# GpSimd's order by hand, one power for several tiles, and a row written to DRAM in 16-byte pieces

One of the cores of a Trainium2 chip runs the whole program. The metric is the device time of one launch in microseconds, the median of several runs; "the kernel before" and "the changed kernel" are the two compared.

## The reference

Two layers over 32 graphs ("batches") of 512 nodes with 512 features and one 512 x 512 adjacency matrix, all in f32. Layer 0 is pre-normalised attention with 8 heads under the adjacency as a mask; layer 1 is a graph attention layer. Cut to what matters:

```python
h = jnp.maximum(_layernorm(x, axis=-1), 0.0)                 # layer 0
q, k, v = h @ Wq + bq, h @ Wk + bk, h @ Wv + bv              # 8 heads of 64
scores = q k^T / 8 + (1.0 - adj) * -1e9
x = x + softmax(scores) @ v @ Wo + bo

h0 = jnp.maximum(_layernorm(x, axis=-1), 0.0)                # layer 1
h = h0 @ W;  s1, s2 = h @ a1, h @ a2
e = leaky_relu(s1[:, :, None] + s2[:, None, :], 0.2) * adj
att = softmax(e, axis=2)
x = x + elu(att @ h + beta * h)
```

## The kernel before

The kernel is software-pipelined over batches. One step of the main loop does, in TensorE's order, the parts of the string `0VD1G2YN3WKQ`: score tiles of head pairs 0 to 3 (digits; each digit also does the products with `v` of the pair before), `V` values, `D` the row sums of layer 1 (`pe`), `G` gather, `Y` layer 1's output, `N` the next batch's transposes, `W` the attention's output projection, `K` and `Q` the next batch's projections. The projections use seven block products instead of eight, fed by sums of blocks ("combinations", `combos`) that GpSimd makes. In the views a product is named after its PSUM tile (`x`, `y` or `qz`) and its part: `y_w` is a product of W, `qz_k` one of K.

TensorE's and VectorE's instructions stand in the order in which the program emits them; the others are placed by the framework's scheduler:

```python
BY_HAND = {mybir.EngineType.PE, mybir.EngineType.DVE}
```

VectorE's small work is put off with `later(key, wait, cost, fn)`, which emits `fn` when a rough clock says that TensorE would not be held up by it.

The combinations; `tT` are those of V, K and Q, `uT` those of W:

```python
def combos(b, name, pairs):
    b11, b12, b21, b22 = (block(pairs, k) for k in range(4))
    t2, t3, t4 = (wtile([P, 2, H], f"{name}{i}_{b}", "T", 5) for i in (2, 3, 4))
    nc.gpsimd.tensor_tensor(t3, b22, b12, op=ALU.subtract)
    nc.gpsimd.tensor_tensor(b12, b12, b11, op=ALU.subtract)
    nc.gpsimd.tensor_tensor(t2, b22, b12, op=ALU.subtract)
    nc.gpsimd.tensor_tensor(t4, t2, b21, op=ALU.subtract)     # "the fourth combination"
    ...
```

The other GpSimd work that matters: `es` (six additions a head pair: the sum of the exponentials), the division `oT`, the residual's constant (`c_row`, four additions a batch), and layer 1's row sums `as`:

```python
def residual(b, st, ...):                       # the start of W
    ...
        nc.gpsimd.tensor_tensor(r[:, t, :], r[:, t, :], c_row, op=ALU.add)

def rest(k):                                    # one "at pair" (two VectorE instructions), its share of as
    z = wtile([P, N], f"at_{b}_{k}", "at", 4)
    nc.vector.scalar_tensor_tensor(z, row, s12[:, 1, k : k + 1], adjT[:, k, :], op0=ALU.add, op1=ALU.mult)
    nc.vector.scalar_tensor_tensor(z, z, ALPHA, z, op0=ALU.mult, op1=ALU.max)
    nc.scalar.activation(z, z, AF.Exp)
    ... nc.gpsimd.tensor_tensor(st["as"], st["as"], z, op=ALU.add)      # for k = 1, 2, 3
```

`row` is `s1` of all 512 nodes on every partition. It comes from a [128, 4] tile by way of DRAM, written element by element and read back as a broadcast:

```python
nc.sync.dma_start(d.rearrange("(t p) -> p t", p=P), col, allow_slow_non_contiguous=True)
nc.sync.dma_start(dst, d.unsqueeze(0).to_broadcast([P, N]))
```

## Time and profile before

| | kernel before |
|---|---|
| time, median (lowest to highest) | 4157.85 us (4149.56 to 4160.77, 4 runs) |
| busy share of the profiled span of 4138.1 us | TensorE 90%, VectorE 57%, GpSimd 54%, ScalarE 34% |
| mean granted TensorE clock | 0.953 |

The prediction below shows the waits and the timelines. Two more lines, from the list of DMA issues (out<-in, queue, count, size, median us from issue to landing):

```profile
s<-row_s SPq DMA_DIRECT2D x32, 256.0 KB, 4.7
...
row_s<-s SPq DMA_DIRECT2D x32, 2.0 KB, 8.0
```

Writing 2 KB takes longer than the 256 KB broadcast that follows. It is on the way of `at`, `as` and `pe`.

### The profile page before, as it was taken

The numbers are of one execution on the slowest core, as the hardware profiler recorded it, in microseconds if no ns is written. First come the engines' busy times: TensorE is split into PE (matmuls) and PEld (weight loads), VectorE is DVE, ScalarE is ACT, GpSimd is POOL, SyncE is SP. The second block draws the span as 40 slices with busy tenths as digits, with TensorE's granted clock in tenths as the row PEclk, the third lists the DMA queues.
The fourth block names the chain that finished last, engine by engine and source line by source line (L and its number), as shares of the span: only waits on it lengthen the run. The fifth ranks groups of instructions, "written<-read, shape, count | busy, mean of one in ns | idle before, by whom it ended". The sixth has DMA issues, their size and how long they took to land. (4 is left out here: it accounts for less than half of the span.)

```text
span 4138.1 us, 59294 instructions
## 1 busy us (share of the span) xinstructions
PE 3735.1 (90%) x24162; PEld 1884.2 (46%) x24162; DVE 2373.7 (57%) x3804; ACT 1404.8 (34%) x2085; POOL 2217.4 (54%) x1922
## 2 busy tenths in 40 slices
PE   6899999999999999999999999999999999999955
PEld 4444444455444444444454444454444454444422
DVE  5566555556565565555666555566555566555553
ACT  2333333333333333333333333333333333333321
POOL 4655465455564555565455564555555555554541
PEclk8999999999999999999999999999999999999978
DMA  3001101011101011010011010011010011010010
GB/s 100 29 4 34 34 31 34 3 34 34 34 31 34 4 34 34 31 34 25 12 34 34 31 34 21 17 34 34 31 34 12 26 34 34 31 34 9 18 34 24
DMA packets 83894, 120.87 MB, mean 29 GB/s; under 512 B 24672, under 2 KB 28768, under 8 KB 83616
## 3 DMA queue, kind: packets, MB, share of 16 engines
q1 hardware_dynamic: 78368, 110.98, 8.4%
q10 hardware_dynamic: 4880, 5.24, 0.4%
q8 instruction: 192, 3.15, 0.4%
q0 software_dynamic: 368, 0.79, 0.1%
q14 instruction: 86, 0.70, 0.1%
HBM read 83.37 MB, written 33.63 MB: 28 GB/s over the span
## 5 line engine op out<-in xcount | busy, mean ns | idle before, releaser
L464 DVE TENSOR_TENSOR e<-ps,nmT 128x1024 f32<-128x1024 f32 x384 | 456.9, 1218 | 751.7 <-PE ps L454 751.7
L475 POOL TENSOR_TENSOR es<-e,e 128x512 f32<-128x512 f32 x256 | 321.6, 1278 | 775.2 <-ACT e L468 775.2
L475 POOL TENSOR_TENSOR es<-es,e 128x512 f32<-128x512 f32 x512 | 681.4, 1363 | 0.0
L468 ACT ACTIVATE e<-e 128x1024 f32<-128x1024 f32 x512 | 541.3, 1057 | 326.9 <-DVE e L464 290.1
L454 PE MATMUL ps<-qT,kT 64*128 64x512 f32 x2048 | 495.0, 618 | 73.5 <-DVE e L464 73.4
L483 PE MATMUL po<-e,v 128*64 128x512 f32 x2048 | 502.8, 635 | 0.1
L46 PE MATMUL py<-w,gT 128*64 128x512 f32 x2048 | 453.1, 595 | 11.3 <-DVE y L646 11.3
L46 PE MATMUL pg<-at,hn 128*64 128x512 f32 x2048 | 451.0, 598 | 3.6 <-DVE dmax L619 3.6
L502 DVE RECIPROCAL rd<-pd 128x512 f32<-128x512 f32 x128 | 428.6, 3348 | 6.7 <-POOL oT L506 6.7
L454 PEld LDWEIGHTS ps<-qT,kT 64*128 64x128 f32 x2048 | 183.4, 187 | 372.1 <-issue 189.1
L406 POOL TENSOR_TENSOR qT<-qT,edge 128x256 f32<-128x256 f32 x128 | 90.4, 727 | 420.7 <-DVE qT L402 420.5
L46 PEld LDWEIGHTS py<-w,gT 128*64 128x64 f32 x2048 | 142.4, 137 | 317.5 <-issue 256.3
L46 PEld LDWEIGHTS pg<-at,hn 128*64 128x64 f32 x2048 | 146.1, 138 | 303.5 <-issue 272.2
L483 PEld LDWEIGHTS po<-e,v 128*64 128x64 f32 x2048 | 157.1, 146 | 272.2 <-issue 246.4
L273 POOL TENSOR_TENSOR rs<-rs,mhalf 128x1 f32<-128x1 f32 x256 | 163.5, 644 | 197.3 <-DVE rs L272 196.8
L588 ACT ACTIVATE at<-at 128x512 f32<-128x512 f32 x128 | 80.7, 630 | 450.7 <-DVE at L587 450.7
L517 POOL TENSOR_TENSOR x<-x,c_row 128x512 f32<-128x512 f32 x128 | 160.0, 1271 | 117.4 <-DMA x<-in_x_dram 112.9
L648 POOL TENSOR_TENSOR y<-y,x 128x512 f32<-128x512 f32 x128 | 161.4, 1271 | 110.7 <-DVE y L646 106.5
L496 ACT COPY oT<-po 128x512 f32<-128x512 f32 x128 | 74.4, 581 | 429.3 <-PE po L483 429.3
L645 DVE TENSOR_SCALAR y<-y 128x512 f32<-128x512 f32 x128 | 123.5, 965 | 145.2 <-ACT y L644 145.2
L46 PE MATMUL qz_k<-hT,wk 128*64 128x256 f32 x512 | 88.9, 505 | 121.3 <-DVE x L528 107.5
L592 POOL TENSOR_TENSOR as<-at,at 128x512 f32<-128x512 f32 x32 | 56.8, 1774 | 256.6 <-ACT at L588 256.6
(179 smaller groups left out, 6051.1 us busy)
## 6 DMA issues: line engine op xcount, KB each, us to landing
x<-in_x_dram SPq DMA_DIRECT2D x128, 256.0 KB, 3.0
x<-in_x_dram SPq DMA_DIRECT2D x64, 512.0 KB, 4.6
out_dram<-y SPq DMA_DIRECT2D x128, 256.0 KB, 2.2
s<-row_s SPq DMA_DIRECT2D x32, 256.0 KB, 4.7
adj<-in_adj_dram SPq DMA_DIRECT2D x4, 256.0 KB, 5.6
w<-in_L_gnn_W_dram ACTq DMA_DIRECT2D x1, 1024.0 KB, 7.5
wk<-in_L_gnn_Wk_dram ACTq DMA_DIRECT2D x3, 256.0 KB, 5.1
wq<-in_L_gnn_Wq_dram ACTq DMA_DIRECT2D x3, 256.0 KB, 7.9
```

Of the source, the lines that this page charges most:

```text
L46: nc.tensor.matmul(out[s : s + HD], lhsT[:, s : s + HD], rhs, start=start, stop=stop, skip_group_check=onto)
L273: nc.gpsimd.tensor_tensor(rstd, rstd, mhalf[:, 0:1], op=ALU.pow)
L406: nc.gpsimd.tensor_tensor(qh, qh, edge8[:, ts(k, H)], op=ALU.mult)
L454: nc.tensor.matmul(ps[s], st["kT"][j][rows, ts(k, P)], st["qT"][j][rows, :], start=True, stop=True)
L464: nc.vector.tensor_tensor(e, p, nmT[:, k, :].unsqueeze(1).to_broadcast([P, 2, N]), op=ALU.add)
L468: nc.scalar.activation(e, e, AF.Exp)
L475: nc.gpsimd.tensor_tensor(es[:, s, :], one[:, s, :], e[:, s, :], op=ALU.add)
L483: nc.tensor.matmul(po[s * HD : (s + 1) * HD, :], v[k // 2][:, k % 2, (2 * j + s) * HD : (2 * j + s + 1) * HD], e[k][:, s, :], start=k == 0 ...
L502: nc.vector.reciprocal(rd, st["pd"])
L517: nc.gpsimd.tensor_tensor(r[:, t, :], r[:, t, :], c_row, op=ALU.add)
L645: nc.vector.tensor_scalar(y, y, 1.0, -1.0, op0=ALU.min, op1=ALU.add)
L648: nc.gpsimd.tensor_tensor(y, y, st["x1"][t // 2][:, t % 2, :], op=ALU.add)
```

## The change

Intent: VectorE and TensorE no longer wait for GpSimd at the wrong moment. (1) GpSimd's order is the order of emission. (2) The power -1/2 of layer norm is taken for all four tiles of a batch (layer 0) or two (layer 1) at once, and layer 0's statistics and normalisation go to other places in VectorE's order. (3) `s1`'s row is written as 128 pieces of 16 bytes; that leaves the queries in the order q*4 + t, so the transposed adjacency is stored in it too, and the diagonal, the row sums and `gT` are read with a step of 16 bytes. The core of the diff:

```diff
-BY_HAND = {mybir.EngineType.PE, mybir.EngineType.DVE}
+BY_HAND = {mybir.EngineType.PE, mybir.EngineType.DVE, mybir.EngineType.Pool}
...
+        if mix:
+            nc.sync.dma_start(d.rearrange("(p t) -> p t", t=T), col)
+        else:
+            nc.sync.dma_start(d.rearrange("(t p) -> p t", p=P), col, allow_slow_non_contiguous=True)
...
+    def mixed(ap):
+        return ap.rearrange("p (q t) -> p t q", t=T)
...
-            nc.scalar.copy(adjT[:, k, :], p)
+            nc.scalar.copy(mixed(adjT[:, k, :]), p.rearrange("p (t q) -> p t q", t=T))
...
+    def root(rstd, mv):
+        nc.vector.tensor_scalar_add(rstd, mv[:, :, 1], EPS)
+        nc.gpsimd.tensor_tensor(rstd, rstd, mhalf[:, : rstd.shape[1]], op=ALU.pow)
...                                                            # norm0, layer 0
-            later(("x", b), 1.2, 0.55, lambda: second(t, mv, rstd))
+            if t == T - 1:
+                root(rstd, mv)
+                for u in range(T):
+                    later(("x", b), 10.0, 0.55, lambda u=u: second(u))
...
-            later(("x", b), 6.0, 1.0, lambda t=t: first(t))
+            later(("x", b), wait, 0.95, lambda t=t: first(t))   # wait is 30 for b > 1
...                                                            # norm1, layer 1: two tiles at once
+            if i:
+                root(rstd, mv)
+                later(key, 2.5, 0.4, second)
...
-        as_row(row, s12[:, 0, :], f"s1_{b}")
+        as_row(row, s12[:, 0, :], f"s1_{b}", mix=True)
...
-            later(("at", b), 5.0, 1.45, lambda k=k: rest(k))
+            later(("at", b), 5.5, 1.45, lambda k=k: rest(k))
...
-            product(nc, pd[:, t, :], st["as"][:, ts(t, P)], ones[:, :HD], start=True, stop=True)
+            product(nc, pd[:, t, :], mixed(st["as"])[:, t, :], ones[:, :HD], start=True, stop=True)
...
-            d = st["at"][k][:, ts(k, P)]
+            d = mixed(st["at"][k])[:, k, :]
...
-        nc.scalar.copy(g, p)
+        nc.scalar.copy(g.rearrange("p (t q) -> p t q", t=T), mixed(p))
```

More of the change, by code (lines that the diff above doesn't have):

```diff
@@ L121, with as_row @@
     dram = ctx.enter_context(tc.tile_pool(name="dram", bufs=2, space=bass.MemoryType.DRAM))
-    def as_row(dst, col, name):
+    def as_row(dst, col, name, mix=False):
         d = dram.tile([N], F32, name=f"row_{name}", tag="row")
-        nc.sync.dma_start(d.rearrange("(t p) -> p t", p=P), col, allow_slow_non_contiguous=True)
+        if mix:
+            nc.sync.dma_start(d.rearrange("(p t) -> p t", t=T), col)
+        else:
+            nc.sync.dma_start(d.rearrange("(t p) -> p t", p=P), col, allow_slow_non_contiguous=True)
         nc.sync.dma_start(dst, d.unsqueeze(0).to_broadcast([P, N]))
+    def mixed(ap):
+        return ap.rearrange("p (q t) -> p t q", t=T)
     nc.vector.memset(fin, 0.0)
@@ L201, in mask @@
             nc.vector.tensor_scalar(m, edge8, -(HD ** 0.5), 1.0, op0=ALU.mult, op1=ALU.add)
-            nc.vector.tensor_tensor(m, adjT[:, k, :], m, op=ALU.max)
+            m_ = m.rearrange("p (t q) -> p t q", t=T)
+            nc.vector.tensor_tensor(m_, mixed(adjT[:, k, :]), m_, op=ALU.max)
             nc.vector.tensor_scalar(nmT[:, k, :], m, -NEG, NEG, op0=ALU.mult, op1=ALU.add)
@@ L266, in row_constants, with stats @@
                 later("wa", 4.0, 0.75, lambda g=g, c=c, ar=ar: dot(g, c, ar))
-    def stats(src, t, u, mv, rstd):
-        st = wtile([P, 6], f"st_{u}_{t}", "st", 4)
+    def stats(src, name, mv):
+        st = wtile([P, 6], f"st_{name}", "st", 4)
         nc.vector.bn_stats(st, src)
         nc.vector.bn_aggr(mv, st)
-        nc.vector.tensor_scalar_add(rstd, mv[:, 1:2], EPS)
-        nc.gpsimd.tensor_tensor(rstd, rstd, mhalf[:, 0:1], op=ALU.pow)
+    def root(rstd, mv):
+        nc.vector.tensor_scalar_add(rstd, mv[:, :, 1], EPS)
+        nc.gpsimd.tensor_tensor(rstd, rstd, mhalf[:, : rstd.shape[1]], op=ALU.pow)
     def load(b):
@@ L282, in load, with norm0, second @@
         return xs
-    def norm0(b, xs):
+    def norm0(b, xs, wait=30.0):
+        mv = wtile([P, T, 2], f"mv0_{b}", "mv0", 2)
+        rstd = wtile([P, T], f"rs0_{b}", "rs0", 2)
         def first(t):
-            mv = wtile([P, 2], f"mv0_{b}_{t}", "mv0", 4)
-            rstd = wtile([P, 1], f"rs0_{b}_{t}", "rs0", 4)
-            stats(xs[t], t, f"a{b}", mv, rstd)
-            later(("x", b), 1.2, 0.55, lambda: second(t, mv, rstd))
-        def second(t, mv, rstd):
+            stats(xs[t], f"a{b}_{t}", mv[:, t, :])
+            if t == T - 1:
+                root(rstd, mv)
+                for u in range(T):
+                    later(("x", b), 10.0, 0.55, lambda u=u: second(u))
+        def second(t):
             nc.vector.tensor_scalar(
-                xs[t], xs[t], mv[:, 0:1], rstd, op0=ALU.subtract, op1=ALU.mult
+                xs[t], xs[t], mv[:, t, 0:1], rstd[:, t : t + 1], op0=ALU.subtract, op1=ALU.mult
             )
         for t in range(T):
-            later(("x", b), 6.0, 1.0, lambda t=t: first(t))
+            later(("x", b), wait, 0.95, lambda t=t: first(t))
     def pair(b, name, p, tag, bufs):
@@ L546, in norm1, with first, second @@
         key = ("hn", b)
-        def first(t):
-            x1, mv = st["x1"][t // 2][:, t % 2, :], st["mv"][:, t, :]
-            rstd = wtile([P, 1], f"rs1_{b}_{t}", "rs1", 4)
-            stats(x1, t, f"b{b}", mv, rstd)
-            later(key, 1.2, 0.16, lambda: second(t, x1, mv, rstd))
-        def second(t, x1, mv, rstd):
-            nb = wtile([P, 1], f"nb_{b}_{t}", "nb", 2)
-            nc.vector.scalar_tensor_tensor(nb, mv[:, 0:1], -1.0, rstd, op0=ALU.mult, op1=ALU.mult)
-            hn = wtile([P, D], f"hn_{b}_{t}", "hn", 4)
-            nc.scalar.activation(hn, x1, AF.Relu, bias=nb, scale=rstd)
-            st["hn"][t] = hn
-            for g, r in ((0, wa1_r), (1, wa2_r)):
-                later(key, 1.8, 0.75, lambda g=g, r=r: third(t, g, r))
+        mv = st["mv"][:, rows[0] : rows[-1] + 1, :]
+        rstd = wtile([P, 2], f"rs1_{b}_{rows[0]}", "rs1", 2)
+        def first(i):
+            t = rows[i]
+            stats(st["x1"][t // 2][:, t % 2, :], f"b{b}_{t}", mv[:, i, :])
+            if i:
+                root(rstd, mv)
+                later(key, 2.5, 0.4, second)
+        def second():
+            nb = wtile([P, 2], f"nb_{b}_{rows[0]}", "nb", 2)
+            nc.vector.scalar_tensor_tensor(nb, mv[:, :, 0], -1.0, rstd, op0=ALU.mult, op1=ALU.mult)
+            for i, t in enumerate(rows):
+                hn = wtile([P, D], f"hn_{b}_{t}", "hn", 4)
+                nc.scalar.activation(
+                    hn, st["x1"][t // 2][:, t % 2, :], AF.Relu,
+                    bias=nb[:, i : i + 1], scale=rstd[:, i : i + 1],
+                )
+                st["hn"][t] = hn
+                for g, r in ((0, wa1_r), (1, wa2_r)):
+                    later(key, 1.5 + i, 0.7, lambda t=t, g=g, r=r: third(t, g, r))
         def third(t, g, r):
@@ L571, in third @@
                 logits(b, st)
-        for t in rows:
-            later(key, 0.0, 1.0, lambda t=t: first(t))
+        for i in range(2):
+            later(key, 0.0, 0.95, lambda i=i: first(i))
     def logits(b, st):
@@ L658, in new_state @@
         }
-        norm0(b, states[b]["x"])
+        norm0(b, states[b]["x"], 30.0 if b > 1 else 6.0)
     def unit(b, j):
```

## The prediction

> **What bounds the kernel now.** I read the page first, then TensorE's waits, then the timeline of one batch engine by engine. The page gives the bound:
>
> ```profile
> PE 3735.1 (90%) x24162; PEld 1884.2 (46%) x24162; DVE 2373.7 (57%) x3804; ACT 1404.8 (34%) x2085; POOL 2217.4 (54%) x1922
> ```
>
> TensorE is busy 90% of the span, and no other engine above 57%. The built programs show that TensorE's order of instructions is the same in both kernels, so the change can act only on TensorE's waits and on the slow clock that follows them. Its waits (us in total, times, longest):
>
> ```profile
> PE pe L46 <- POOL as L594: 134.9, 32, 38.0
> PE qz_k L46 <- DVE x L528: 107.5, 28, 4.5
> PE ps L454 <- DVE e L464: 73.4, 32, 3.6
> ```
>
> Three waits, once a batch each, are nearly all of it: the row sums `pe` of layer 1 wait for GpSimd's `as`, the first K projection waits for VectorE's last residual addition, the fourth score tile waits for VectorE. TensorE's timeline of one batch (start, length, and in brackets the idle time before):
>
> ```profile
> 2009.45 3.63 PE L483 MATMUL po<-e,v 128*64 128x512 f32 x16
> ...
> 2013.87 2.85 PE L454 MATMUL ps<-qT,kT 64*128 64x512 f32 x12
> 2018.76 1.13 PE L454 MATMUL ps<-qT,kT 64*128 64x512 f32 x4 [2.04 <-DVE e L464]
> ...
> 2035.95 0.69 PE L46 MATMUL pe<-ones,as 128*64 128x64 f32 x16 [3.31 <-POOL as L594]
> ...
> 2040.86 3.70 PE L454 MATMUL ps<-qT,kT 64*128 64x512 f32 x16
> ...
> 2087.14 3.70 PE L454 MATMUL ps<-qT,kT 64*128 64x512 f32 x16
> 2090.77 1.95 PE L46 MATMUL x_w<-wo,oT 128*64 128x256 f32 x16
> ...
> 2101.64 1.90 PE L46 MATMUL qz_w<-wo,uT 128*64 128x256 f32 x16
> 2103.37 1.90 PE L46 MATMUL x_k<-hT,wk 128*64 128x256 f32 x16
> 2108.85 3.43 PE L46 MATMUL qz_k<-hT,wk 128*64 128x256 f32 x16 [3.58 <-DVE x L528]
> ```
>
> From end of Q to end of Q a batch takes 123.56 us here; over the steady stretch of the timeline, 124.9. I cut it in five: Q's end to `pe` 26.5 (mean of all batches 26.8), `pe` to the gather 8.5 at full clock and 10.2 after a clock drop (mean 9.8), then 46.3 in every batch, W and K 30.15 (mean 29.9), Q 12.1. GpSimd's timeline explains two of these:
>
> ```profile
> 2016.92 1.77 POOL L592 TENSOR_TENSOR as<-at,at 128x512 f32<-128x512 f32 x1 [6.98 <-ACT at L588]
> ...
> 2023.54 5.87 POOL L475 TENSOR_TENSOR es<-es,e 128x512 f32<-128x512 f32 x4
> ...
> 2048.10 4.96 POOL L475 TENSOR_TENSOR es<-es,e 128x512 f32<-128x512 f32 x4
> ...
> 2092.90 2.50 POOL L517 TENSOR_TENSOR x<-x,c_row 128x512 f32<-128x512 f32 x2 [2.12 <-DMA x<-in_x_dram]
> 2095.36 2.50 POOL L475 TENSOR_TENSOR es<-e,e 128x512 f32<-128x512 f32 x2
> ```
>
> The scheduler has put two of the three `as` additions ahead of `es`, and the residual's constant (`c_row`) ahead of the `es` of head pair 3. In between, from 2016.9 until `pe` may start, GpSimd is almost never idle: `pe` waits for a full queue.
>
> [...] L587, which reads `at` twice, takes 0.69 us with GpSimd idle and 1.65 beside it, and the six `es` additions take 8.31 us (2021.07 to 2029.38) beside one L584/L587 pair against 7.40 (2045.63 to 2053.03) without. GpSimd thus loses 0.91 a pair. [...] after 3.58 us idle the `qz_k` group took 3.43 us and not 1.90, and the next 2.20. Waits of 2 us do it in some batches too. [...]
>
> **The change, part by part.**
>
> *One power for several tiles.* Eight powers and eight additions of epsilon a batch become three. GpSimd saves 5 x 0.64 = 3.2 us, VectorE 5 x 0.15 plus two `nb`; neither bounds there. What counts is that norm 0's statistics leave the W stretch. VectorE there stood 4.13 us at `x L292`, waiting for a power behind GpSimd's full queue, with the residual additions behind it; that was the cause of the `qz_k` wait. This wait, 3.36 us a batch (107.5/32), goes away, if the additions can run.
>
> *Row in 16-byte pieces.* 128 pieces in place of 512. My estimate for landing, from the 2.2 us of the 256 KB output writes with 128 rows, is 2.3 us instead of 8.0. The last dot now stands behind the first Q evacuation (which ended at 2005.46) and ends, with its own 0.61, about 3.4 us before Q's end and no longer 8.4; the broadcast (4.3 in 2001.03 to 2013.31, less 8.0) then brings the row 3.2 us after Q's end. Only one `at` stands before the scores (1.45 us), done at 4.65; the first score tile needs VectorE at 5.6. The `ps` wait (73.4/32 = 2.3 us) should vanish. In the drain at the end two row writes lie on the only chain: 2 x 5.7 = 11 us saved.
>
> *GpSimd's order by hand.* The built order is now: `es`, the division, four combinations, then three `as`; and in W's stretch four combinations, `es`, the division, and only then the four `c_row` additions. I follow both queues.
>
> Q's end to `pe`: the scores start 4.42 us after Q's end, `es` 4.77 later (2040.86 to 2045.63), so 9.2. Then `es` 7.40, division 1.35, four combinations 4 x 1.35 = 5.4, three `as` 3 x 1.25 = 3.75: 17.9. VectorE now does three `at` pairs beside this chain (before: one, and half of another): 3 x 0.91 = 2.7. Sum 29.8 against 26.8: **+3.0 us**. V itself has ended by about 22.4 (VectorE's `at` work may also hold its last group some 2 us, hidden here), so the `ps` wait saved is paid back in `pe`. After so long a wait the clock is always down: 10.2 for 9.8, **+0.4**.
>
> W and K: `es` of pair 3 starts at 2087.14 + 4.77 = 2091.9, ends 2099.3; division 2100.6; four `c_row` at 1.25: the first pair done 2103.1, the second 2105.6. W's fifth product can only be read by VectorE (0.69) after that, at 2106.4, and W's seventh, in the same PSUM, starts then and not at 2101.64: a new wait of 4.8 us. `qz_k` waits no more. From there eight groups of 1.73 are left, and up to 1.7 us for the slow clock: 2106.45 + 13.8 + 1.7 = 2121.95, which is 31.2 after W's start, 31.0 on average as the drop may miss a batch. Against 29.9: **+1.1**.
>
> Sum: +4.5 us a batch, over 30 full batches +135; drain -11, and some 2 for the start either way: 4158 + 135 - 11 = 4282, rounded to 4280.
>
> *Mixed order.* The strided reads (`gT`'s copy from PSUM, `as` as weights, the diagonal) have a step of 16 bytes; the copies have 2.8 us of slack in the gather. The 16 weight loads of `pe` may take longer; I put 0 for it, with up to 1 us a batch in the range.
>
> **The rivals.**
> (a) *The author's aim holds*: GpSimd runs ahead, as it no longer stands 7 us at `as` while `es` data are ready (6.98 in its timeline), and both VectorE waits disappear. All three waits with their clock drops are near 13 us a batch; a third of it gained would give 4158 - 130 = 4030. Against it: the three `as` and the `c_row` now stand last in a queue that I find full to the end.
> (b) *No net effect*: contention costs GpSimd nothing extra (then 27.1 for 29.8), and W's wait only takes the place of `qz_k`'s. Then +1.8 a batch, 4158 + 54 - 11 = 4200, within 2%.
> (c) *Worse than I say*: the row write stays near 8 us. Then `at` holds the first scores by almost 5 us, the `ps` wait returns on top, and the time goes beyond 4340. A quarter of the pieces speaks against it.
>
> **Range and chances.** The W wait and the length of GpSimd's chain are sums of measured durations in an order that is known; the contention (0 to 4 us) and the clock drops (1 us either way) are not. One us a batch is 30 us. So 4205 to 4330. The 2% line is at 4241: 0.74 for slower, 0.16 for the same, 0.10 for faster, the last since a tuned kernel's next version is seldom this much worse.
>
> **What would show it.** Right: `pe <- POOL as` of 6 to 8 us a batch; `qz_w <- DVE x L544`-type waits near 4.8 us where `qz_k`'s were, with VectorE waiting there for GpSimd's `c_row`; `ps <- DVE e` near zero; row landing 2 to 3 us. Wrong: `pe` waits under 4 us, or `c_row` done before W's fifth product, or a row landing over 6 us.

Cut from it are three rules stated more widely than any run of this case shows; no term of its sum goes with them: +3.0, +0.4 and +1.1 are +4.5 us a batch, times 30 is +135, and 4158 + 135 - 11 = 4282. The 8.0 us of the row's write are in the view above. The 0.91 us of GpSimd for an `at` pair comes from one pair of stretches of the trace before, so 2.7 for three is an estimate. The up to 1.7 for the slow clock is what 10.2 is above 8.5. "Always down": in the trace before, the two longest waits of `pe` (37.95 and 30.94 us, in the drain) were followed by a `pe` of 1.12 us at a clock of 0.50, where it took 0.69 at 1.00; in the changed kernel all 32 waits of `pe` (4.59 to 28.91 us) were followed by one of 1.22 or 1.23. "Waits of 2 us": one of 1.89 us ahead of the fourth score tile was followed by an `x_v` group of 3.28 us at a clock of 0.57, one of 2.04 by one of 1.95. Of the 28 waits of `qz_k` (3.35 to 4.48 us) 8 were followed by a group of 1.95 us, so a drop can miss a batch.

## The result

| | before | changed |
|---|---|---|
| time, median (lowest to highest) | 4157.85 us (4149.56 to 4160.77) | 4472.75 us (4469.53 to 4472.98) |
| ratio, 95% interval | | 1.0759 (1.074 to 1.0778) |
| profiled span, mean clock | 4138.1 us, 0.953 | 4471.0 us, 0.928 |

A ratio here is the mean time of one kernel's fast runs over that of the other's of the same rounds, so not quite the ratio of the medians that are quoted. The changed kernel is 7.6% slower; slower by 3% was foretold, and the range ended at 4330.

TensorE's waits in the changed kernel (us in total, times, longest):

```profile
PE qz_w L46 <- DVE x L544: 314.5, 31, 10.5
PE pe L46 <- POOL as L618: 267.9, 32, 28.9
PE qz_v L46 <- DVE v L456: 38.7, 29, 1.4
...
PE ps L470 <- DVE e L480: 6.0, 2, 5.4
```

The wait for scores is gone (73.4 to 6.0), the one of `qz_k` too. `pe` waits twice as long as before (134.9 to 267.9), and W's last product has a new wait of 10 us a batch. VectorE's addition that it waits for waits in turn for GpSimd's constant:

```profile
DVE x L544 <- POOL x L533: 439.8, 61, 12.9
```

To place the time I cut a batch at five marks of TensorE's timeline, as the prediction did; means over the steady batches, in us:

| | Q's end to `pe` | `pe` to gather | gather to W | W and K | Q | batch |
|---|---|---|---|---|---|---|
| before | 26.8 | 9.8 | 46.3 | 29.9 | 12.1 | 124.8 |
| foretold | 29.8 | 10.2 | 46.3 | 31.0 | 12.1 | 129.4 |
| changed | 29.7 | 10.9 | 46.3 | 37.6 | 12.1 | 136.5 |

The 29 steps that run the whole string are 336 us longer together, what comes ahead of them (with the first W) 12 longer, and what follows 15 shorter; that is the +333 of the spans. Four of the five stretches are as foretold within 0.7 us, and one, W and K, is not. GpSimd's timeline of that stretch in the changed kernel (start, length, in brackets the idle time before and what ended it):

```profile
2118.99 1.27 POOL L327 TENSOR_TENSOR tT<-hT,hT 128x512 f32<-128x512 f32 x1
2120.34 1.26 POOL L328 TENSOR_TENSOR hT<-hT 128x512 f32<-128x512 f32 x1
2121.68 1.26 POOL L329 TENSOR_TENSOR tT<-hT,hT 128x512 f32<-128x512 f32 x1
2131.45 1.27 POOL L330 TENSOR_TENSOR tT<-tT,hT 128x512 f32<-128x512 f32 x1 [8.51 <-PE y_w L46]
2132.68 2.50 POOL L491 TENSOR_TENSOR es<-e,e 128x512 f32<-128x512 f32 x2
2135.14 4.93 POOL L491 TENSOR_TENSOR es<-es,e 128x512 f32<-128x512 f32 x4
2140.02 1.26 POOL L522 TENSOR_TENSOR oT<-oT,rd 128x512 f32<-128x512 f32 x1
2141.24 4.92 POOL L533 TENSOR_TENSOR x<-x,c_row 128x512 f32<-128x512 f32 x4
```

and TensorE's in the same batch, with `pe` ahead of it, whose wait of 7.34 us is as foretold:

```profile
2068.27 1.22 PE L46 MATMUL pe<-ones,as 128*64 128x64 f32 x16 [7.34 <-POOL as L618]
...
2121.80 3.70 PE L470 MATMUL ps<-qT,kT 64*128 64x512 f32 x16
2125.43 1.95 PE L46 MATMUL x_w<-wo,oT 128*64 128x256 f32 x16
...
2129.34 1.95 PE L46 MATMUL y_w<-wo,uT 128*64 128x256 f32 x16 [0.24 <-ACT y_w L376]
...
2146.94 3.68 PE L46 MATMUL qz_w<-wo,uT 128*64 128x256 f32 x16 [10.47 <-DVE x L544]
2150.41 2.46 PE L46 MATMUL x_k<-hT,wk 128*64 128x256 f32 x16
```

GpSimd stands 8.51 us ahead of the fourth `tT` combination, for W's product `y_w`. That product reads a `uT` tile, and of the tiles with tag `T` there are five: three of `uT` and two of `tT` fill them, so the sixth gets its buffer when `y_w` has read the first. The program emits this combination in N, long before W; by hand, it also stands there in GpSimd's queue, and `es` of pair 3, the division and the residual's constant stand behind it. W's last product then waits for VectorE, which waits for the constant. In the kernel before the scheduler had put the same combination behind the division:

```profile
2103.20 1.27 POOL L506 TENSOR_TENSOR oT<-oT,rd 128x512 f32<-128x512 f32 x1
2104.43 1.26 POOL L314 TENSOR_TENSOR tT<-tT,hT 128x512 f32<-128x512 f32 x1
```

### The profile page after: what moved, and what is told of

It reads as the page before. It is cut to its first block, busy times and chain, and to the rows that moved or that the text cites. A ratio compares the mean times of both kernels' runs of the same rounds, so it can differ in the third digit from the quotient of the medians.

```text
span 4471.0 us, 58887 instructions
## 1 busy us (share of the span) xinstructions
PE 3754.7 (84%) x24162; PEld 1798.7 (40%) x24162; DVE 2419.8 (54%) x3580; ACT 1401.4 (31%) x2085; POOL 2158.4 (48%) x1762
## 3 DMA queue, kind: packets, MB, share of 16 engines
q1 hardware_dynamic: 66080, 110.98, 7.7%
## 4 chain that ended last, share of the span: by engine, by line
PE 57%; POOL 21%; DVE 12%; issue 4%; ACT 4%; DMA 1%; DVEq 0%; ACTq 0%; POOLq 0%; SPq 0%
PE po L499 11%; PE pg L46 10%; POOL es L491 9%; PE py L46 5%; PE ps L470 5%; DVE e L480 4%; PE qz_q L46 4%; PE qz_k L46 4%; POOL x L533 3%; ACT e L484 3%; PE x_k L46 3%; PE qz_w L46 3%; DVE e L477 3%; DVE rd L518 2%; PE pd L506 2%
## 5 line engine op out<-in xcount | busy, mean ns | idle before, releaser
L491 POOL TENSOR_TENSOR es<-es,e 128x512 f32<-128x512 f32 x512 | 667.7, 1335 | 0.0
L499 PE MATMUL po<-e,v 128*64 128x512 f32 x2048 | 522.4, 657 | 0.1
L470 PE MATMUL ps<-qT,kT 64*128 64x512 f32 x2048 | 475.9, 603 | 6.0 <-DVE e L480 6.0
L46 PE MATMUL qz_w<-wo,uT 128*64 128x256 f32 x1024 | 175.0, 502 | 314.5 <-DVE x L544 314.5
L285 POOL TENSOR_TENSOR rs<-rs,mhalf 128x2 f32<-128x2 f32 (+1 forms) x96 | 88.0, 917 | 557.1 <-DVE rs L284 525.0
L46 PE MATMUL pe<-ones,as 128*64 128x64 f32 x512 | 39.2, 331 | 267.9 <-POOL as L618 267.9
L544 DVE SCALAR_TENSOR_TENSOR x<-x_w,x 128x512 f32<-128x512 f32 x32 | 22.1, 692 | 413.6 <-POOL x L533 385.0
L46 PEld LDWEIGHTS qz_w<-wo,uT 128*64 128x64 f32 x1024 | 90.6, 178 | 382.1 <-DVE x L544 328.6
L376 ACT COPY y_k<-x_k 128x512 f32<-128x512 f32 x32 | 18.3, 571 | 605.1 <-PE x_k L46 522.2
```

The costliest lines, as they stand in the source:

```text
L46: nc.tensor.matmul(out[s : s + HD], lhsT[:, s : s + HD], rhs, start=start, stop=stop, skip_group_check=onto)
L470: nc.tensor.matmul(ps[s], st["kT"][j][rows, ts(k, P)], st["qT"][j][rows, :], start=True, stop=True)
L491: nc.gpsimd.tensor_tensor(es[:, s, :], one[:, s, :], e[:, s, :], op=ALU.add)
L499: nc.tensor.matmul(po[s * HD : (s + 1) * HD, :], v[k // 2][:, k % 2, (2 * j + s) * HD : (2 * j + s + 1) * HD], e[k][:, s, :], start=k == 0 ...
```

## The experiments

**Theory A**: the loss comes from GpSimd's order by hand, in W's stretch, from the combination's wait for a buffer and from the constant's late place behind `es`. **Theory B**: the strided reads of the mixed order cost it. **Theory C**: the late `as` additions carry most of it. Ten kernels were run, all with results equal to the reference's, three rounds each against the kernel before. The kernel before itself had medians of 4172.6 (e1 to e4), 4173.2 (e5 to e8) and 4143.8 us (e9, e10) on the chips used; so compare by ratio across these groups. The diffs are cut to the lines that matter; e6 contains e5, e7 contains e6, and e8 contains e7. The stretches are those of the table above; gather to W was 46.3 and Q 12.1 in every one but e10.

| | us | ratio to before (95%) | Q's end to `pe` | `pe` to gather | W and K | batch |
|---|---|---|---|---|---|---|
| before | 4157.85 | 1 | 26.8 | 9.8 | 29.9 | 124.8 |
| changed | 4472.75 | 1.0759 (1.0740 to 1.0778) | 29.7 | 10.9 | 37.6 | 136.5 |
| e1 changed, GpSimd scheduled | 4089.25 | 0.9805 (0.9788 to 0.9821) | 29.5 | 10.5 | 25.1 | 123.4 |
| e2 hand order alone | 4447.95 | 1.0652 (1.0608 to 1.0696) | 29.1 | 10.7 | 37.7 | 135.9 |
| e3 16-byte row alone | 4069.20 | 0.9754 (0.9737 to 0.9770) | 24.1 | 10.2 | 30.4 | 123.0 |
| e4 one power alone | 4237.46 | 1.0157 (1.0140 to 1.0174) | 33.8 | 10.7 | 25.1 | 127.9 |
| e5 changed, fourth `tT` after W | 4271.57 | 1.0242 (1.0220 to 1.0265) | 29.8 | 10.6 | 31.0 | 129.7 |
| e6 e5, constant ahead of `es` | 4112.91 | 0.9862 (0.9840 to 0.9883) | 29.8 | 10.6 | 25.3 | 124.0 |
| e7 e6, `uT` after `pe` | 3969.21 | 0.9518 (0.9496 to 0.9539) | 25.5 | 10.4 | 25.3 | 119.5 |
| e8 e7, three `at` first | 3789.46 | 0.9084 (0.9063 to 0.9104) | 20.6 | 8.9 | 25.5 | 113.4 |
| e9 e8, GpSimd scheduled | 3928.82 | 0.9480 (0.9459 to 0.9500) | 24.0 | 10.4 | 25.0 | 117.7 |
| e10 changed, sixth buffer | 4321.21 | 1.0430 (1.0407 to 1.0452) | 29.7 | 10.9 | 31.7 | 131.5 |

### The three parts, one at a time

**e1**, all of the change but the first line:

```diff
-BY_HAND = {mybir.EngineType.PE, mybir.EngineType.DVE, mybir.EngineType.Pool}
+BY_HAND = {mybir.EngineType.PE, mybir.EngineType.DVE}
```

> The changed kernel with GpSimd's order given back to the scheduler; one power for several tiles and the 16-byte row stay. The built order then has the residual's constant ahead of es of pair 3 and the fourth combination tT behind the division, as in the kernel before, while the three row-sum additions stay late. Theory A (the loss is GpSimd's hand order, in W's stretch: its queue stands 8.5 us at the fourth tT combination, which needs a buffer that W's third product frees, and es and the residual's constant stand behind it): W and K fall from 37.6 to about 24.6 us a batch, Q's end to pe stays near 29.5, so about 4095 us. Theory B (the strided reads and the mixed order cost it): stays near 4470. Theory C (the late row-sum additions carry most of the loss): over 4350.

4089.25 us: the other two parts together are a gain of 2.0%, with the same strided reads. Theory B falls. W and K are 25.1, so all of W's loss goes with the hand order. Q's end to `pe` is as long as in the changed kernel (29.5 and 29.7): what is lost there does not need the hand order, and theory C's share is the smaller one, 2.9 of the 11.7 us a batch.

**e2**, the kernel before with that line as in the changed kernel:

```diff
-BY_HAND = {mybir.EngineType.PE, mybir.EngineType.DVE}
+BY_HAND = {mybir.EngineType.PE, mybir.EngineType.DVE, mybir.EngineType.Pool}
```

> The kernel before with one line changed: GpSimd's order by hand. Theory A: the whole loss is here: W and K about 38 us a batch (the wait at the fourth tT combination and, behind it, VectorE's wait for the powers), Q's end to pe about 28 (one combination ahead of the last row-sum addition): near 4450 us. Theory B (the mixed order): near 4180. Theory C: about 4200.

4447.95 us, 6.5% slower by one line, with W and K at 37.7. (Its 29.1 ahead of `pe` is made up in another way: the row still lands late, in 8.7 us, and the score wait is there, 103.0 us in all.) The wait in W is the same one; GpSimd's waits in e2:

```profile
POOL tT L314 <- PE y_w L46: 251.9, 30, 8.5
```

**e3**, the kernel before with the 16-byte row and all reads that go with it:

```diff
-        as_row(row, s12[:, 0, :], f"s1_{b}")
+        as_row(row, s12[:, 0, :], f"s1_{b}", mix=True)     # and mixed() as in the change
```

> The kernel before with the row in 16-byte pieces and the order of queries that it gives, nothing else. GpSimd's built order is that of before. Theory A: the row lands 5 to 6 us earlier, the score wait vanishes, the first two row-sum additions come ahead of es without a wait, Q's end to pe falls from 26.8 to about 24.5: about 4070 us. Theory B (strided weights, diagonal, copies from PSUM cost more than the row gives): 4170 or more.

4069.20 us. The write lands in 1.4 us instead of 8.0, as the list of DMA issues of e3 shows; its queue moved 66080 packets instead of 78368, and the difference is 32 times the 384 pieces saved:

```profile
s<-row_s SPq DMA_DIRECT2D x32, 256.0 KB, 4.0
...
row_s<-s SPq DMA_DIRECT2D x32, 2.0 KB, 1.4
```

The score wait disappears and `pe` comes 2.7 us earlier.

**e4**, one power for several tiles with its new places, the row in 4-byte pieces, GpSimd scheduled:

```diff
 # the changed kernel, less mix=True and every mixed(), less Pool in BY_HAND
-            later(("at", b), 5.5, 1.45, lambda k=k: rest(k))
+            later(("at", b), 5.0, 1.45, lambda k=k: rest(k))
```

> The kernel before with one power for several tiles and its new places in VectorE's order, the row in 4-byte pieces, GpSimd scheduled. W and K lose their wait: about 24.6 us a batch instead of 29.9. But the last dot now ends 3.4 us before Q's end, so with a row that takes 8 us VectorE stands at the first at ahead of the scores until 9 us after Q's end: es, and with it pe, come near 5 us later (Q's end to pe 34). Sum about 4240 us. If the row's duration does not matter: about 4095, as e1.

4237.46 us, 1.6% slower. W and K win 4.8 us, and Q's end to `pe` loses 7.0, since VectorE now stands at the first `at` for the slow row, ahead of the scores:

```profile
DVE at L607 <- DMA s<-row_s: 190.6, 32, 13.4
...
PE ps L469 <- DVE e L479: 122.9, 31, 5.4
```

The second and third part of the change thus need each other: the late dots (VectorE's products that give `s1` and `s2`) can only be afforded with the fast row. The power itself and its new places were not run apart. Together (e1) they are still no better than the row alone (e3: 0.9754, e1: 0.9805). What W wins is lost again ahead of `pe`, where two `at` pairs more stand behind the scores (24.1 becomes 29.5; e9 below has three pairs ahead of the scores again, its GpSimd scheduled, and 24.0).

### Which instructions in GpSimd's queue

**e5**, one instruction of the changed kernel emitted later:

```diff
-        nc.gpsimd.tensor_tensor(t4, t2, b21, op=ALU.subtract)
+        last = lambda: nc.gpsimd.tensor_tensor(t4, t2, b21, op=ALU.subtract)   # tT: called after W
```

> The changed kernel with one GpSimd instruction moved: the fourth tT combination, which waits for a buffer that W's third product frees, is emitted after W instead of ahead of es of pair 3. The residual's constant still stands behind es and the division. If the missed term of the prediction was that buffer wait and nothing else, W and K come to the 31.0 us that the prediction worked out (a wait of 4.8 us before W's last product) instead of 37.6: 4473 - 6.6 x 30 = 4275 us. If the wait is due to something else in W's stretch, it stays above 4400.

4271.57 us, W and K 31.0: what the prediction had for that stretch, with a wait of 4.48 us where 4.8 was foretold:

```profile
2044.77 3.60 PE L46 MATMUL qz_w<-wo,uT 128*64 128x256 f32 x16 [4.48 <-DVE x L550]
```

Moving one instruction of 1.3 us in each batch took some 200 us off. The missed term is this one.

**e10** asks the same with the order left alone, and takes away what makes the combination wait:

```diff
-        t2, t3, t4 = (wtile([P, 2, H], f"{name}{i}_{b}", "T", 5) for i in (2, 3, 4))
+        t2, t3, t4 = (wtile([P, 2, H], f"{name}{i}_{b}", "T", 6) for i in (2, 3, 4))
-        y = wtile([P, D], f"y_{b}_{t}", "y", 3)
+        y = wtile([P, D], f"y_{b}_{t}", "y", 2)          # and the others of this tag: to make room
```

> The changed kernel, GpSimd's order untouched, with a sixth buffer for the combinations instead of five; to make room, y has two buffers instead of three, which costs time in the stretch with layer 1's output (some 3 us a batch, as the third exponential waits for the first output write). The fourth tT combination then waits for no product. If the buffer is what made GpSimd stand: W and K 31.0 us as in e5, and 4275 + 30 x 3 = 4365 us. If the place in the order mattered in another way: W and K stay at 37.6 and the time goes beyond 4473.

4321.21 us. GpSimd no longer waits for `y_w`, W and K are 31.7, and W's last product waits less than half as long as in the changed kernel:

```profile
PE qz_w L46 <- DVE x L544: 135.4, 31, 5.0
```

The smaller `y` cost 0.9 us a batch (gather to W 47.2), not the 3 us that I had expected. So the buffer, and not the place as such, made GpSimd stand.

**e6**, the residual's constant ahead of the scores of pair 3:

```diff
-        }.get(b, "0VD1G2YN3WKQ")
+        }.get(b, "0VD1G2YNR3WKQ")        # R: residual(b - 1, prev), taken out of W
```

> e5, and the four additions of the residual's constant emitted ahead of the scores of pair 3, so ahead of its es in GpSimd's queue. Theory A: W's wait disappears, W and K 25 us, as in e1, while Q's end to pe stays 29.7: 4473 - 12.6 x 30 = 4095 us, equal to e1 within 1%. So hand order as such costs nothing; the place of five instructions does. If hand order costs something of its own: 4150 or more.

4112.91 us, W and K 25.3. By ratio it is 0.6% slower than e1 (0.9862 and 0.9805), which is within what was expected; hand order as such costs next to nothing.

**e7**, `uT` after the row sums:

```diff
-        if j == NP - 1:
-            st["oT"] = combos(b, "uT", st["o"])
...
-        }.get(b, "0VD1G2YNR3WKQ")
+        }.get(b, "0VDU1G2YNR3WKQ")       # U: prev["oT"] = combos(b - 1, "uT", prev["o"])
```

> e6, and the four uT combinations (wanted only in W) emitted after the row sums' matmuls instead of ahead of the three as additions. Q's end to pe: GpSimd has 6.3 us less ahead of as, but the last at is ready 23.9 after Q's end, so 25.3 instead of 29.7: 4095 - 4.4 x 30 = 3965 us. If VectorE's work in V and not GpSimd's queue sets pe: stays near 4095.

3969.21 us: Q's end to `pe` fell from 29.8 to 25.5. In e6 it was GpSimd's queue that set `pe`.

**e8** joins the two halves that the change had traded against each other:

```diff
-                    later(("x", b), 10.0, 0.55, lambda u=u: second(u))
+                    later(("x", b), 40.0 if b > 2 else 10.0, 0.55, lambda u=u: second(u))
-            later(("at", b), 5.5, 1.45, lambda k=k: rest(k))
+            later(("at", b), 4.0, 1.45, lambda k=k: rest(k))
```

> e7, and layer 0's four normalisations moved from before the scores to after the next pair's, and three at pairs ahead of the scores as in the kernel before. With the row landed about 1 us after Q's end they are done at 5.3, ahead of the first score tile (5.6); GpSimd's chain is then es 9.2 to 17.5, division 18.8, last as 20.1, just about V's end at 20.3. All three waits of the kernel before gone: per batch 20.4 + 9 + 46.3 + 24.7 + 12.1 = 112.5 instead of 125: 4158 - 12.5 x 30 = 3780 us. If at again holds the scores, or the row comes later: 3850 to 3960.

3789.46 us, 9.2% less time than the kernel before and some 16% less than the changed one. Its two edits were not run apart. Busy times and TensorE's longest waits of e8:

```profile
PE 3622.9 (96%) x24162; PEld 1784.4 (47%) x24162; DVE 2559.5 (68%) x3580; ACT 1401.1 (37%) x2085; POOL 2153.8 (57%) x1762
```

```profile
PE pe L46 <- POOL as L622: 52.8, 2, 29.1
PE py L46 <- DVE y L674: 11.5, 30, 0.7
```

`pe` waits only in the two drain steps, TensorE is busy 96% of the span, and its mean granted clock was 0.984 (0.953 before).

**e9**, e8 with the scheduler back:

```diff
-BY_HAND = {mybir.EngineType.PE, mybir.EngineType.DVE, mybir.EngineType.Pool}
+BY_HAND = {mybir.EngineType.PE, mybir.EngineType.DVE}
```

> e8 with GpSimd's order given back to the scheduler. The built orders differ in a batch by two things: the last as addition stands behind three uT combinations instead of ahead of them, and the first half of the residual's constant ahead of the last layer 1 addition. Theory A (only the places of these few instructions count): pe waits some 4 us again (3 x 1.35), with a clock drop of up to 1.7: 3789 + 30 x 5 = 3940 us. If hand order brings nothing by itself: 3789 within 1%.

3928.82 us, and 0.9480 against e8's 0.9084. The scheduler puts the last `as` behind three combinations again, and `pe` comes 3.5 us later; the stretch behind it, where a clock drop of up to 1.7 was expected, takes 10.4 us for 8.9. Here the hand order is worth 4%: it gains or loses by the order that one writes.

## Why the prediction was wrong

- *TensorE's order is the same, so only its waits and clock count*: held, but for what the strided weights of `pe` cost (below).
- *The `qz_k` wait goes with the power; the score wait goes with the row*: both held (neither is left among TensorE's waits but for 6.0 us). The row landed in 1.4 us, not 2.3.
- *Q's end to `pe` 29.8*: 29.7. The sum, with 0.91 us lost by GpSimd for each `at` pair beside it, was right to 0.1, and so was its main part: from the first `es` to the last `as` GpSimd took 20.45 us in the batch shown, for 17.9 + 2.7 foretold. The wait of VectorE's addition in V (1.4 us, foretold as up to 2) was hidden behind this chain.
- *`pe` to gather 10.2, strided weights put at 0*: 10.9. The instructions of `pe` in the kernel before and then in the changed one (shortest/median/longest ns):

```profile
L46 PEld LDWEIGHTS pe<-ones,as x512: 132/138/232, 283.0 to 4096.3; 128*64 128x64 f32 x171
L46 PE MATMUL pe<-ones,as x512: 222/222/366, 283.0 to 4096.4; 128*64 128x64 f32 x171
```

```profile
L46 PEld LDWEIGHTS pe<-ones,as x512: 193/217/217, 292.9 to 4429.0; 128*64 128x64 f32 x171
L46 PE MATMUL pe<-ones,as x512: 322/324/381, 292.9 to 4429.1; 128*64 128x64 f32 x171
```

  These medians are of different clocks: the clock granted in the `pe` of the batches shown was 1.00 before and 0.50 in the changed kernel. Two more groups of `pe` part the two causes, one of e4 (no step; at the clock of 0.50 the kernel before took the same 1.12 us) and one of e8 (with the step; the `po` behind it took 3.60 us, as in the kernel before at 1.00):

```profile
2085.90 1.12 PE L46 MATMUL pe<-ones,as 128*64 128x64 f32 x16 [6.40 <-POOL as L617]
```

```profile
2094.20 1.07 PE L46 MATMUL pe<-ones,as 128*64 128x64 f32 x16
```

  At full clock the step costs 0.4 us a batch (1.07 for 0.69), at half clock 0.1 (1.22 for 1.12). e2 and e4, without the step, also have 10.7 in this stretch. So most of the missing 0.7 lies in the slow clock after the wait, for which 10.2 was too little (`po` behind `pe` took 5.46 us in the batch shown, 3.60 in the batch shown of the kernel before). Of the other reads with a step of 16 bytes, the diagonal's update on VectorE took 449 ns for 346 (medians), and ScalarE's copy of `gT` from PSUM 586 for 585.

- *W and K: "`es` of pair 3 starts at 2087.14 + 4.77 = 2091.9"*: **this is the step that failed.** It took GpSimd to be free when the first exponentials were there, counting the durations ahead of `es` but not the waits. The fourth combination ahead of it cannot start until W's own third product has run. Counted as the prediction counted, `es` would have started at 2121.80 + 4.77 = 2126.6 in the batch shown above; it started at 2132.7. That 6.1 us and 0.6 more lost to the clock (after the wait of 10.47 us W's last product took 3.68 us and the group behind it 2.46, for 1.90 each in the kernel before: 2.3 lost where up to 1.7 was foretold) make, within 0.1, the 6.6 between 31.0 and 37.6. Times 30, as the prediction counted, it is 198 us, and the 0.7 ahead of the gather adds 21; less 7 for start and drain (by this count 18 us shorter, where 11 was foretold), and less 18 because the profiled run of before (4139.84 us) was that much below its median, it is about the 193 us by which the prediction missed. e5 takes the wait away, and the foretold 31.0 is there; so, nearly, is the whole sum (ratio 1.0242, where 4280 would be 1.029).
- *The rivals*: (a), a gain from hand order, did not come in the changed kernel, yet e8 and e9 show that it was to be had; (b) fell; (c) did not happen, as the row was fast, but e4 shows its mechanism: with the slow row the score wait returns.

The wait could have been seen ahead: the instruction stood ahead of `es` in the built order, its output shares five buffers with a set of six, and the timeline before shows it 15 us later than its three sisters. I read the order of the queue and not each entry's condition.

## What to carry to other kernels

When an engine goes over to the order of emission, check for every instruction in its queue what it waits for, buffers included: one that waits for a later part of the pipeline stops all behind it, and here 13.6 us of work stood behind a subtraction of 1.3. Emit work by when its result is wanted, not by when its inputs are there: the row sums ahead of combinations that are wanted much later, the residual's constant ahead of sums that nobody reads yet. And a change of three parts that gives and takes in the same stretch should be measured part by part: here one part alone saved 2.5%, another alone cost 6.5%, and the third won 4.8 us in one stretch and lost 7.0 in another.
